# Layer-0 attention of a fused transformer kernel: ScalarE in written order, LayerNorm applied in halves, expert tiles that end at an expert's last row

## The chip, the cores and the metric

The kernel runs on one core of one Trainium2 chip. The metric is the device time of one launch in microseconds. A core has five engines with instruction streams of their own: TensorE (PE in the profile, its weight loads apart as PEld), VectorE (DVE), ScalarE (ACT), GpSimd (POOL) and SyncE (SP), which here only issues DMAs.

## What is computed

The reference has four stages over `x`, 16 sequences of 512 rows with 128 values:

```python
x = x + _L0_attn_ref(_layernorm(x), w_attn, b_attn, w_proj, b_proj)   # causal, 16 heads of 8
x = x + _L0_ffn_ref(_layernorm(x), Wg, bg, W1, b1, W2, b2)            # 8 experts, the best 2 of each row
x = x + _L1_attn_ref(_layernorm(x), w_Q, w_K, w_V)                    # full attention, 16 heads of 8
x = x + _L1_ffn_ref(_layernorm(x), w_gate, w_up, w_down)              # gated FFN on values rounded to FP4
```

In the second stage the gate takes the two largest of eight logits of a row, and only those two experts count for it.

## The kernel before

**Stages.** `attention(0)` runs the causal attention of all 16 batches and, behind each batch, the gate of the experts. It sends every row of the normalised `x` (with three more values, so `ROW` = 131 floats) to a table `x_rows` in DRAM by an indirect DMA of GpSimd, once for each of its two experts. Expert `e` owns `CAP` = 8704 rows of that table from row `e * CAP` on, and its rows lie one behind the other. `plan_tiles` then forms up to `NT` = 39 tiles of `TS` = 512 rows, and `moe`, which `attention(1)` calls, loads one tile after another with its expert's weights. `gated_ffn` ends the kernel.

**The loop of `attention(0)`.** A group is one batch and one of four sets of heads, so there are 64 groups. A group has four steps, one for each chunk `kc` of 128 keys, and a batch has 16 steps; below, "phase" is a step's place in the 16 of a batch, so phase 4 is `kc` 0 of the second group. A step issues in Python order: what hangs in `soon`; the first score matrix for the row maxima of the group three ahead (`row_max`: matmuls `ps_max`, VectorE maximum `mx`); the first score matmuls `ps_sc` with their exponentials `pt` on ScalarE (`score`, L825) and a causal mask on GpSimd; what hangs in `later`; the other half of the maxima and of the scores, for `kc` 0 and 1 only; what hangs in `last_of`; and the value matmuls `ps_av` of the step before (`attend`).

**Work hung into the steps.** For a batch two ahead the prologue has the parts `stats`, `moments`, `scale` (LayerNorm: the shift `nm` on VectorE, then four ScalarE instructions that write `xn`), `turn` (transposes, and a ScalarE copy `xnT`), `both` (for each of q and k a matmul `ps_qk` and a ScalarE instruction `hi`), `low` (VectorE, `lo`), and the spreading of q and k over strips by SP's DMAs (`first`, `second`). `put_max` transposes the maxima, ScalarE copies them to `mT` (L796), and four DMAs of SP (L798) put them into the q strips; `ps_sc` needs that. `gate_after` hangs the gate of a finished batch: `stats`, `moments`, `scale` (here ScalarE writes `xg`, L217), `turned`, the logits `ps_g`, and at every second batch a chain of small VectorE instructions that ends with the sends.

**What sets the order.** Tile's scheduler orders the instructions of each engine by priorities and its cost model, except where the kernel ties them. `in_order` ties an instruction behind the last one of its queue. TensorE is tied throughout, GpSimd mostly (its sends are `passing`: other work may pass them). `vec`, a `Lane`, ties VectorE as long as "dve" is in `strict`, which is so for `attention(0)`. ScalarE is not tied: it runs in the order that the scheduler has chosen. Two rings of PSUM buffers matter: `for_dve` (2 buffers of two banks: `ps_max`, `ps_qk`, `ps_g`, `ps_d`, `ps_n`, `ps_o`) and `for_act` (4 buffers: `ps_sc`, `ps_av`, `ps_t`, `ps_mx`, `ps_v`).

**Zero rows.** The tiles of an expert start at multiples of 512 rows, so its last tile reads past its last row. `clear_steps`, hung behind batch 13, has SP read the fill of each expert from `ends_at` and write 1536 zero rows (786 KB) behind it. The first DMA of it, of 262 KB, belongs to tiles beyond the plan.

## Time and profile before

| what | us |
|---|---|
| median of 3 runs (2483.97 to 2493.26) | 2490.11 |
| the profiled execution | 2510.72 |
| its span | 2509.0 |
| from the start to the first `ps_av` | 68.6 |
| batches 0 to 14 of `attention(0)` | 68.6 to 909.2 |
| last batch, to the last output projection | 909.2 to about 959 |
| last gate, sends and plan, to the first expert's transposes | about 959 to 996 |
| experts | 996 to about 1344 |
| `attention(1)` | to about 2208 |
| `gated_ffn` | to 2509 |

A row "A <- B: total, times, longest" of the waits gives the idle time of an engine just before instruction A that ended when B was done. A row of the timeline is start, duration, engine, line, operation, output and inputs, and in brackets the idle time before it with what ended it. A row of the windows has the busy time of each engine in a stretch, the granted clock of TensorE (1.00 is full speed) and the busy share of the DMA engines. The matmuls all have line L267 or L270 and VectorE's tied work L180, lines of helpers, so one goes by the tiles' names.

### The profile page before, as it was taken

The page shows a single profiled execution, that of the slowest core. Times are in us where ns is not written, and L with a number is a line of the kernel's source. Part 1 is how long each engine was busy: PE and PEld are TensorE (multiplying, and loading weights), DVE is VectorE, ACT ScalarE, POOL GpSimd, SP SyncE. Part 2 cuts the span into 40 slices and gives each one's busy share as a digit, 9 for nine tenths or more (in the row PEclk, how much of TensorE's full clock was granted, in tenths as well). Part 3 has the DMA queues.
Part 4 walks back from the last instruction along what each step waited for, and adds up shares of the span by engine and source line. Part 5 has one row for each costly group of instructions (what it writes and reads, how often), then busy time and mean ns, then how long its engine had stood idle before and what let it go on. Part 6 is the DMA issues. An engine that isn't in the chain of part 4 may idle for free.

```text
span 2509.0 us, 38679 instructions
## 1 busy us (share of the span) xinstructions
PE 2167.2 (86%) x13324; PEld 1077.6 (43%) x13324; DVE 1703.2 (68%) x3106; ACT 1388.2 (55%) x2716; POOL 886.1 (35%) x1384
## 2 busy tenths in 40 slices
PE   6998999999999983989998898999889999957776
PEld 2444444444444441656674333333333333325554
DVE  5666565566656546956435777777777778679887
ACT  1655555455555452333334777777777777854443
POOL 3333544445354446032002333322233331045553
PEclk8999898799999785999999999999999999978888
DMA  6112222122121255445552222222222221000000
GB/s 184 55 54 80 78 62 62 62 63 80 61 71 61 63 78 95 137 139 164 155 151 63 61 79 82 82 63 62 62 65 84 75 81 54 2 1 17 17 18 17
DMA packets 156930, 184.48 MB, mean 74 GB/s; under 512 B 25647, under 2 KB 120976, under 8 KB 148544
## 3 DMA queue, kind: packets, MB, share of 16 engines
q1 hardware_dynamic: 147806, 164.55, 23.3%
q0 software_dynamic: 8352, 17.20, 2.5%
q8 instruction: 107, 1.75, 0.3%
q14 instruction: 87, 0.71, 0.1%
q10 hardware_dynamic: 578, 0.26, 0.1%
HBM read 116.55 MB, written 63.28 MB: 72 GB/s over the span
## 4 chain that ended last, share of the span: by engine, by line
PE 65%; DVE 19%; ACT 7%; POOL 4%; issue 3%; DMA 2%; SPq 1%; POOLq 0%; ACTq 0%; DVEq 0%
PE ps_av L267 17%; PE ps_max L267 15%; PE ps_sc L267 11%; DVE mx L772 7%; PE ps_h L267 4%; PE ps_y L267 4%; ACT pt L825 3%; PE ps_qk L267 3%; PE ps_gu L267 2%; PE ps_t L270 2%; PE ps_d L270 2%; PE ps_v L267 1%; DVE q_t L1172 1%; PE ps_mx L270 1%; PE ps_o L267 1%
## 5 line engine op out<-in xcount | busy, mean ns | idle before, releaser
L772 DVE TENSOR_REDUCE mx<-ps_max 128x2 f32<-128x1024 f32 (+1 forms) x896 | 1012.7, 1147 | 436.9 <-PE ps_max L267 389.8
L825 ACT ACTIVATE pt<-ps_sc 128x512 f32<-128x512 f32 (+2 forms) x1792 | 900.3, 569 | 479.1 <-PE ps_sc L267 454.9
L267 PE MATMUL ps_sc<-q,k 64*128 64x512 f32 (+3 forms) x2048 | 485.1, 422 | 78.3 <-ACT pt L825 57.5
L267 PE MATMUL ps_av<-pt,va 128*32 128x512 f32 (+3 forms) x4096 | 503.8, 560 | 4.6 <-ACT pt L825 1.1
L267 PE MATMUL ps_max<-k,q 64*128 64x512 f32 (+3 forms) x2048 | 446.3, 453 | 33.5 <-DVE mx L772 24.5
L830 POOL TENSOR_SCALAR_AFFINE_SELECT pt<-pt 128x128 f32<-128x128 f32 (+1 forms) x768 | 248.3, 331 | 468.8 <-ACT pt L825 450.3
L267 PEld LDWEIGHTS ps_max<-k,q 64*128 64x128 f32 x2048 | 193.5, 196 | 469.1 <-issue 200.8
L267 PEld LDWEIGHTS ps_sc<-q,k 64*128 64x128 f32 x2048 | 229.6, 195 | 223.8 <-ACT pt L825 121.3
L1291 ACT ACTIVATE h<-ps_h,b1t 128x512 f32<-128x512 f32 x156 | 107.0, 687 | 194.9 <-PE ps_h L267 194.2
L267 PE MATMUL ps_h<-xT,w1t 128*128 128x512 f32 x312 | 151.3, 617 | 3.4 <-DVE xT L278 1.8
L267 PE MATMUL ps_y<-w2t,h 128*128 128x128 f32 x1248 | 148.7, 278 | 6.3 <-DVE yt L1305 6.3
L267 PEld LDWEIGHTS ps_av<-pt,va 128*32 128x32 f32 x4096 | 85.6, 111 | 146.1 <-issue 94.7
L267 PEld LDWEIGHTS ps_y<-w2t,h 128*128 128x128 f32 x1248 | 144.5, 194 | 8.9 <-DVE yt L1305 6.7
L1225 POOL DMA_INDIRECT got<-y_rows,backs x128 | 124.1, 969 | 63.0 <-issue 32.7
L532 POOL DMA_INDIRECT x_rows<-xg,slots x128 | 126.2, 986 | 27.5 <-issue 27.3
L267 PE MATMUL ps_max<-mask_bf,ident_bf 128*128 128x128 bf16 (+1 forms) x768 | 133.5, 260 | 0.0
L239 POOL TENSOR_TENSOR ln_rstd<-ln_ve,mhalf 128x4 f32<-128x4 f32 x32 | 34.5, 1078 | 255.0 <-DVE ln_nm L241 252.0
L267 PE MATMUL ps_gu<-wgT,xqT 128*128 128x352 f32 x128 | 67.0, 613 | 62.0 <-DVE hid L1418 33.2
L681 POOL TENSOR_TENSOR lo<-full,hi 128x512 fp32r<-128x512 f32 x32 | 40.9, 1280 | 150.4 <-ACT hi L679 150.4
L267 PE MATMUL ps_qk<-xnT,wp 128*128 128x512 f32 x128 | 75.8, 675 | 13.8 <-ACT hi L675 12.5
L270 PE MATMUL ps_d<-cst,av_sb 128*128 128x128 f32 x512 | 85.6, 291 | 1.4 <-ACT av_sb L856 1.4
L267 PEld LDWEIGHTS ps_h<-xT,w1t 128*128 128x128 f32 x312 | 51.2, 192 | 77.8 <-ACT h L1291 53.3
(205 smaller groups left out, 2317.5 us busy)
## 6 DMA issues: line engine op xcount, KB each, us to landing
q<-d SPq DMA_DIRECT2D x256, 128.0 KB
k<-d SPq DMA_DIRECT2D x256, 128.0 KB
d<-hi SPq DMA_DIRECT2D x64, 256.0 KB
d<-lo SPq DMA_DIRECT2D x64, 256.0 KB
xt<-x_rows SPq DMA_DIRECT2D x39, 262.0 KB
w1t<-in_w_dram SPq DMA_DIRECT2D x39, 256.0 KB
w2t<-in_w_dram SPq DMA_DIRECT2D x39, 256.0 KB
y_rows<-yt SPq DMA_DIRECT2D x39, 256.0 KB
```

Source lines behind the costliest of these rows:

```text
L239: in_order(nc.gpsimd.tensor_tensor(rstd, ve, mhalf, ALU.pow), queue="pool")
L267: return in_order(nc.tensor.matmul(out, lhsT, rhs, start=start, stop=stop))
L270: return in_order(nc.tensor.transpose(out, src, ident))
L532: ins = in_order(nc.gpsimd.indirect_dma_start(out=x_rows[:, :], out_offset=bass.IndirectOffsetOnAxis(ap=slots[:, b0 + u, k, c : c + 1], axis=0
L681: nc.gpsimd.tensor_tensor(lo, full, hi.bitcast(F32), ALU.subtract),
L772: nc.vector.tensor_reduce(hv["mx"][:, c, :, p0 : p0 + m], s4, AX.X, ALU.max),
L825: nc.scalar.activation(pt[:, 0 : m * n], ps[:, 0 : m * n], AF.Exp, scale=SCALE)
L830: nc.gpsimd.affine_select(head, head, pattern=[[0, m], [1, P]], base=0, channel_multiplier=-1, compare_op=ALU.is_ge, fill=0.0,),
L1172: nc.vector.scalar_tensor_tensor(t, r, MAGIC, v, ALU.add, ALU.add)
L1225: ins = in_order(nc.gpsimd.indirect_dma_start(out=got[:, c, :], out_offset=None, in_=y_rows[0 : min(NT, NE * (b + 1)) * TS, :], in_offset= ...
L1291: nc.scalar.activation(h[:, f, :], ps, AF.Gelu, bias=t["b1"][:, f : f + 1])
```

## The change

1. ScalarE gets a `Lane` too (`act`), and `strict` holds "act" beside "dve" in `attention(0)`: ScalarE runs in written order there.
2. `scale` becomes `shift` (VectorE's `nm`) and `apply0`, `apply1` (two ScalarE instructions each). In the prologue they hang at phases 1, 1 and 2 in place of 3; in the gate at phase 8 (after the step's last exponentials) and phase 9 in place of all at phase 8.
3. `both` issues the two matmuls `ps_qk` first and then the two `hi` (`high`), where it was matmul, `hi`, matmul, `hi`.
4. The gate's later parts are spread over more steps: the transposes at phase 11, the logits at phases 12 and 13 (were 10 and 11), the choice from phase 14 on (was 12), `fill` once for each batch, sends one step later. Four of batch 14's eight sends hang three steps earlier.
5. The start is rewritten: batch 0's LayerNorm, transposes and q, k come ahead of `pattern`, `strips` and `bias_rows`. Only batch 2's `x` is fetched before the loop; each later one is fetched in the loop, nine steps ahead of its `stats`.
6. An expert's last tile starts at its fill less 512 rows (or at 0), so it ends at its last row and overlaps the tile before. `clear_steps` goes. `clear` writes 512 zero rows at the start of each of the eight regions and of a ninth, at every second step from 6 to 22. `plan_tiles` and `places_back` get the extra arithmetic.

```diff
-    vec = Lane(nc.vector, "dve")
+    vec, act = Lane(nc.vector, "dve"), Lane(nc.scalar, "act")
...
+        def apply(part):
...
+            for c in range(NC // 2 * part, NC // 2 * (part + 1)):
+                act.activation(
                     to[:, c, 0:E], xb[:, c, :], AF.Identity,
-                    bias=nm[:, c : c + 1], scale=rstd[:, c : c + 1],
+                    bias=st["nm"][:, c : c + 1], scale=st["rstd"][:, c : c + 1],
                 )
...
-        vec.tensor_scalar(row, who[:, :, 0], float(CAP), None, ALU.mult)
-        vec.scalar_tensor_tensor(row, kth[:, :, 0], float(TS), row, ALU.mult, ALU.add)
+        vec.tensor_scalar(code, who[:, :, 0], -1.0, float(NE), ALU.mult, ALU.add)
+        vec.tensor_tensor(
+            has[:, 1 - v], rev.to_broadcast(wide), code.unsqueeze(2).to_broadcast(wide),
+            ALU.is_equal,
+        )
+        mine = pool.tile(wide, F32, name="mine", tag="xg", bufs=3)
+        vec.tensor_tensor(
+            mine, has[:, 1 - v], held.rearrange("p e o -> p o e").to_broadcast(wide), ALU.mult
+        )
+        vec.tensor_reduce(spot, mine, AX.X, ALU.add)
+        vec.tensor_scalar(spot, spot, -float(TS), 0.0, ALU.add, ALU.max)
+        vec.tensor_scalar(kth, kth, float(TS), None, ALU.mult)
+        vec.tensor_tensor(row, kth[:, :, 0], spot[:, :, 0], ALU.min)
+        vec.scalar_tensor_tensor(row, who[:, :, 0], float(CAP), row, ALU.mult, ALU.add)
...
-    def clear_steps():
...
+    def clear(e):
+
+        nc.sync.dma_start(
+            out=rows_of(x_rows, slice(e * CAP, e * CAP + TS)),
+            in_=zeros.to_broadcast([P, TS // P, ROW]),
+        )
...
-            strict.add("dve")
+            strict.update(("dve", "act"))
...
-                    nc.scalar.activation(hi, ps, AF.Identity, bias=bp[:, t : t + 1])
                     return
...
+            def high(t):
+                ps, hi, lo = st["split", t]
+                act.activation(hi, ps, AF.Identity, bias=bp[:, t : t + 1])
...
-                    both=lambda: (split(0), split(1)), low=lambda: (low(0), low(1)),
+                    both=lambda: (split(0), split(1), high(0), high(1)),
+                    low=lambda: (low(0), low(1)),
...
             run(0, "stats", "moments")
             weights_turned()
+            run(0, "shift", "apply0", "apply1", "turn", "both")
             pattern()
             strips(0)
             run(1, "stats", "moments")
+            run(0, "low", "first")
             bias_rows()
-            run(0, "scale", "turn", "both", "low", "first")
+            run(1, "shift", "apply0", "apply1", "turn", "both")
             value_columns(0)
-            run(0, "values")
             strips(1)
-            run(0, "second")
-            run(1, "scale", "turn", "both", "low")
+            run(0, "values", "second")
+            run(1, "low")
...
-            for b in range(2, B):
-                in_order(fetch(b), queue="sp")
+            in_order(fetch(2), queue="sp")
+            for b in range(3, B):
+                later.setdefault(NC * G * (b - 2) - 14, []).append(lambda b=b: fetch(b))
+            for e in range(NE + 1):
+                later.setdefault(6 + 2 * e, []).append(lambda e=e: clear(e))
...
-                    ("stats", -5, last_of), ("moments", -1, last_of), ("scale", 3, later),
-                    ("biased", 4, later), ("turn", 5, later), ("both", 7, later),
-                    ("low", 7, last_of), ("first", 9, later), ("values", 11, later),
-                    ("second", 16, later),
+                    ("stats", -5, last_of), ("moments", -1, last_of), ("shift", 1, later),
+                    ("apply0", 1, last_of), ("apply1", 2, last_of), ("biased", 4, later),
+                    ("turn", 5, later), ("both", 7, later), ("low", 7, last_of),
+                    ("first", 9, later), ("values", 10, later), ("second", 16, later),
...
+            if ng == 2:
+                steps = (
+                    (1, 2), (2, 2), (4, 1), (4, 2), (5, 2), (7, 1), (8, 2), (9, 2), (10, 0),
+                    (10, 1), (11, 1), (12, 1), (13, 1), (14, 0), (14, 1), (15, 1), (15, 1),
+                )
...
+                    if b == B - 2:
+
+
+                        at = NC * len(groups) - step + (3 if m >= len(rows) // 2 else 0)
...
+            nc.vector.tensor_scalar(held, held, -float(TS), 0.0, ALU.add, ALU.max)
```

In `steps` the first number is a distance from the step in which the batch is finished (phase 4), the second says `soon` (0), `later` (1) or `last_of` (2).

## The prediction

> **What bounds the kernel now.** I read the windows by stage first. From the first `ps_av` to the last batch TensorE is busy 778.8 of 840.6 us, VectorE 511, ScalarE 468, GpSimd 372: TensorE carries the stage, and what can be won is its 61.8 us of idle time and its clock.

> ```profile
> 68.60:909.20 840.60, 778.79 (x5545) 373.02 (x5543) 510.96 (x1065) 468.48 (x1013) 372.47 (x858) 0.90 0.21 64
> ...
> 957.60:996.00 38.40, 5.05 (x24) 3.70 (x23) 25.58 (x89) 2.44 (x6) 26.56 (x24) 0.50 0.16 48
> ```

> Next, TensorE's waits from 65 to 930 us. They sum to nearly all of that idle time, and four rows come once in each of 13 or 14 batches, always with the same length: this is no noise but one place in the schedule, met again and again.

> ```profile
> PE ps_sc L267 <- ACT pt L825: 31.0, 14, 2.2
> PE ps_qk L267 <- ACT hi L675: 10.9, 14, 0.8
> PE ps_max L267 <- DVE lo L180: 8.0, 14, 0.6
> PE ps_o L267 <- ACT aT L278: 7.3, 13, 0.6
> ```

> The timeline of batch 3 (phase 8) shows the largest. ScalarE's four `xg` stand ahead of the exponentials `pt`; they wait for `ln_nm`, which VectorE makes only after `lo` and `mx`; so `pt` is late by 2.7 + 1.65 us although its `ps_sc` was done at 247.0, and TensorE runs out of `for_act` buffers.

> ```profile
> 248.77 1.65 ACT L217 ACTIVATE xg<-x,ln_nm,ln_rstd 128x128 f32<-128x128 f32 x4 [2.68 <-DVE ln_nm L180]
> 250.33 2.05 ACT L825 ACTIVATE pt<-ps_sc 128x512 f32<-128x512 f32 x4
> ...
> 250.95 0.79 PE L267 MATMUL ps_sc<-q,k 64*128 64x512 f32 x1 [2.21 <-ACT pt L825]
> ```

> The windows around it show what follows: TensorE is busy 1.51 of 3.41 us, and then its clock is 0.50 for three such stretches. The same eight value matmuls take 1.06 us at full clock and 1.93 at half.

> ```profile
> 246.66:250.07 3.41, 1.51 (x7) 0.53 (x7) 3.21 (x5) 1.30 (x4) 0.00 (x0) 1.00 0.74 262
> 250.07:253.49 3.42, 2.54 (x15) 1.19 (x15) 0.18 (x1) 2.89 (x6) 2.10 (x5) 0.50 0.76 220
> ...
> 214.39 1.06 PE L267 MATMUL ps_av<-pt,va 128*32 128x512 f32 x8
> ...
> 256.43 1.93 PE L267 MATMUL ps_av<-pt,va 128*32 128x512 f32 x8
> ```

> Last, the ends of the stage, in the timelines of SP and TensorE. At 59.66 the four `mT` DMAs come out behind 14 fetches of `x` (11.2 us of issue) and TensorE waits 4.0 us for them; at 917.62 they stand among the zero rows and it waits 7.5 us.

> ```profile
> 48.34 11.21 SPq L84 DMA_DIRECT2D x<-in_x_dram  x14
> 59.66 2.38 SPq L798 DMA_DIRECT2D q<-mT  x4
> ...
> 911.67 5.14 SPq L384 DMA_DIRECT2D x_rows<-zeros  x3
> 917.62 5.18 SPq L798 DMA_DIRECT2D q<-mT  x4
> 924.23 20.64 SPq L384 DMA_DIRECT2D x_rows<-zeros  x5
> ...
> 931.28 1.19 PE L267 MATMUL ps_sc<-q,k 64*128 64x512 f32 x3 [7.54 <-DMA q<-mT]
> ```

> **The change part by part**, against the profiled 2510.7 us.

> 1. *`apply` in halves, behind the exponentials, ScalarE in written order.* At phase 8 no exponential stands behind `xg` any more; the next ones meet at most two of its instructions (0.9 us), while `nm` has long been made. Gone: 31.0. `xn` leaves phase 3, where it stood ahead of `aT`: gone 7.3.
> 2. *Both `ps_qk` ahead of both `hi`.* The second matmul doesn't wait for the first `hi`: gone 10.9. `lo` comes about 1.8 us sooner, but it still holds one of two `for_dve` buffers: I leave 0.4 of each 0.57 us, gone 2.4. Bounds: 0 to 8.0. Together 51.6 us.
> 3. *The clock.* A mean of 0.90 over 840.6 us is 840.6 x 0.2 = 168 us at half clock. Between the pairs 1.06/1.93 and 0.44/0.69 (two `ps_sc` of 384) I take a factor of 1.6, so each such us gives back 0.375: 63 us. Nearly every period begins in the window of the 2.2 us wait. I take four fifths as gone, 50; bounds 0 and 63. Two periods are long (416 to 465 us at 0.55, 820 to 857 at 0.54, together 78 us where two usual ones are 15): 24 us of the 63 belong to that, and explain that the profiled execution is 20.6 us above the median.
> 4. *New waits.* `ps_g` now holds a `for_dve` buffer from the end of phase 12 to phase 14, over a step with two maxima (phase 13); before it was over `kc` 3, which has one. The second `ps_max` there then waits for the first's `mx` (0.96 us less the 0.44 of `ps_sc` between, and a delay): 0.6 us, 16 times, 9.6. `ps_n` at phase 1 and the exponential of the gate (`g_d`) between two sets at phase 0 cost some 0.2 and 0.3, 8 times: 4. In all 13.6 lost; bounds 0 and 28 (twice that), as no row shows them.
> 5. *The choice from phase 14 on* takes five VectorE instructions of 0.22 us from between the two maxima of `kc` 0. VectorE has 330 us to spare: 0.
> 6. *No zero rows at the end.* The 7.5 us wait goes, and 13.7 us at half clock behind it, 13.7 x 0.375 = 5.1: 12.6. The `mT` written at 917.0 would land at about 921.8 by the 4.2 us of the first, ahead of need at 923.7.
> 7. *Zero rows at the start.* Nine DMAs of 262 KB, 0.44 us of SP each, at the 160 GB/s of the old ones 1.6 us of transfer each, one in two steps of some 5.5 us. Behind them on SP stand q and k of batch 2, needed only after the lead of three groups, 12 steps; and `mT`. Cover: that lead. 0; up to 4 if one `mT` meets them.
> 8. *Fetches in the loop.* Nine steps, over 25 us, ahead of need: 0. At the start `mT` leaves SP at once: 4.0 gone.
> 9. *The start.* `nm` waits no longer for `ps_b` and `b_bc`: ScalarE's first `xn` came at 13.09, `ln_rstd` was there at 8.4, so it can begin near 8.6, and the chain to the first `ps_max` moves by 4.5 us, with paired matmuls by some 6.5. VectorE waits 1.5 us for `rstd` with `pat`, `k` and batch 1's `stats` behind it, all of which have time before 25. Gone 6.5; bounds 3 and 8.
> 10. *The tail.* The last gate's chain (VectorE, from `x` at 958.85 to the sends at 973.84) sets it, then eight sends at 1.26 us. GpSimd now has four more sends ahead of the last `ln_rstd`, which had 2.4 us of idle: 0 to 1.3 lost. The plan gets six more small VectorE instructions (0.2 to 0.5 us each); its end already stands behind `wp`, which waits for the sends, and there such instructions took 0.2 or, beside GpSimd's memsets, 1.7 to 1.8 us. `mine` takes a third buffer of the `xg` ring, which may have to wait for the last sends. I take 2 lost; bounds -3 (`wp` placed better) and +9.
> 11. *`places_back`* gets three small instructions under the experts' matmuls (TensorE busy 323 of 344 us): 0. The number of tiles stays 39.

> Sum: 51.6 + 50 + 12.6 + 4.0 + 6.5 - 13.6 - 2 = 109, so 2510.7 - 109 = 2402 us. The median lacks most of the excess of the two long periods (0.8 x 24 = 19 of the 109): 2490.1 - 90 = **2400 us**.

> **Rivals.**
> - *The waits go, the slow clock stays* (another window per batch is too empty, at `ps_g` in phase 13 say). For it: two long periods run through windows in which TensorE is busy all the time. Against: windows busy 0.77 kept their clock. 50 and 5.1 drop out, with the 19: 2490.1 - (51.6 - 13.6 + 7.5 + 10.5 - 2) = 2436. Chance 0.13.
> - *VectorE becomes the bound*: at the new pace `ps_max` waits for `mx`, 2 us in each of 14 batches: 2428. Against: 511 us of work in some 750. Chance 0.08.
> - *Written order turns on ScalarE* (slower). If `ln_rstd` on GpSimd is late for `nm`, VectorE and ScalarE both stand, in written order, with `mx` and the exponentials behind them. In the steady batches `nm` came 4.7 to 8.4 us after `rstd`; the prologue's moves forward by two steps (2.8 + 2.4 us), so some 2 to 3 us are left, and sends of 0.97 us lie on GpSimd between. It ends slower from 90 / 14 = 6.4 us per batch on: a wait of 3.6 with a slow period of 10.2 (3.8) gives 2400 + 14 x 7.4 = 2504. Chance 0.06.
> - *The change does little*: the exponentials stay late for another reason, as the buffers of `pt`, and only start and end are won: 2490 - 23 + 14 = 2481. Chance 0.03.

> **How the numbers follow.** The likeliest case has 0.70. With all bounds good it ends at 2364; the second rival ends at 2436; the range is 2360 to 2445, which leaves out the last two. A measurement here tells about 0.5% (12 us) from no change. Faster by more 0.91, within 0.03, slower 0.06.

> **What would show it.** In the profile after, the four rows above shrink to under a fifth, except `lo`; the clock from the first `ps_av` to the last batch is 0.97 or more; a batch takes some 49 us, not 55; the first `ps_max` starts near 27 us, not 33.7; no wait for `mT` over 1 us; the experts start 36 to 40 us after the last output projection, as now. It is wrong if `ps_sc` waits for ScalarE at another phase, if `ps_max` waits more than 28 us more for `mx`, or if the clock stays at 0.90.

## The result: 2447 us, less than half of the forecast gain

| run | before, median us | after, median us | ratio, 95% interval |
|---|---|---|---|
| first comparison | 2487.11 | 2447.00 (2441.59 to 2449.80) | 0.9833, 0.9805 to 0.9861 |
| the same two kernels again (`after_again`, on the first chip of the experiments) | 2503.80 | 2484.09 (2471.27 to 2497.52) | 0.9906, 0.9871 to 0.9942 |

The change is faster by 40 us in one comparison and by 20 us in the other. The forecast was 90. 2447 lies 2 us above its range. Here and below, a ratio leaves out executions more than 1.5% above the fastest one of the same kernel.

The stages of the two profiled executions, cut at the same matmuls (first `ps_av`, last batch, last `ps_o`, first and last expert matmul, last `ps_sc` of `attention(1)`):

| stage | before | after | difference | forecast |
|---|---|---|---|---|
| start | 68.6 | 64.1 | -4.5 | -10.5 |
| batches 0 to 14 | 840.6 | 805.7 | -34.9 | -88.0 |
| last batch | 49.6 | 49.9 | +0.3 | -12.6 |
| tail (last gate, sends, plan) | 40.1 | 41.9 | +1.8 | +2.0 |
| experts | 345.2 | 343.7 | -1.5 | 0 |
| `attention(1)` | 860.8 | 833.8 | -27.0 | 0 |
| `gated_ffn` | 304.2 | 300.8 | -3.4 | 0 |

The four changed stages lose 37.3 us together, about what the medians say. The spans differ by 69.2 us, but 27.0 of that is `attention(1)`, whose instructions stand in the same order in both kernels. It took 835.2 to 835.7 us in all four kernels profiled on one chip below, and 852.0 to 856.4 us in all twelve profiled on two others: this difference doesn't belong to the change. The record doesn't name the chips of the two profiles above. Since 860.8 is near the slower group and 833.8 near the faster, they were probably not taken on one chip, and the other rows may hold a part of such a difference too: in `after_again` batches 0 to 14 took 823.1 us, 17.5 less than before and not 34.9.

The windows of the batches, after. The columns are length, then busy time and count of TensorE, its weight loads, VectorE, ScalarE and GpSimd, then granted clock, DMA share and GB/s.

```profile
64.10:869.80 805.70, 771.39 (x5543) 376.89 (x5541) 509.99 (x1058) 465.90 (x1013) 372.50 (x858) 0.90 0.22 67
```

TensorE's idle time fell from 61.8 to 34.3 us. The clock did not move: 0.896 before, 0.902 after. That is 174.6 us at half clock before and 157.8 after, and 199.4 in `after_again`. TensorE's work, 778.8 us before, takes 771.4 us.

TensorE's waits from 65 to 900 us, after:

```profile
PE ps_max L273 <- DVE lo L180: 16.1, 14, 1.1
PE ps_max L273 <- DVE mx L770: 13.4, 24, 0.7
PE ps_sc L273 <- ACT pt L180: 5.3, 7, 3.1
PE ps_sc L273 <- ACT av_sb L180: 1.8, 7, 0.3
```

The rows for `hi` and `aT` are gone, and `pt` at phase 8 with them. The row of `lo` doubled, and `mx` is new. The timeline of batch 6 shows why `lo` is late:

```profile
403.27 1.98 PE L273 MATMUL ps_qk<-xnT,wp 128*128 128x512 f32 x4
405.30 1.26 ACT L180 ACTIVATE hi<-ps_qk,bp 128x512 fp32r<-128x512 f32 x2 [1.20 <-PE ps_qk L273]
406.60 1.41 DVE L180 SCALAR_TENSOR_TENSOR lo<-ps_qk,bp,hi 128x512 fp32r<-128x512 f32 x2 [2.89 <-ACT hi L180]
408.06 0.49 PE L273 MATMUL ps_max<-k,q 64*128 64x512 f32 x2 [1.15 <-DVE lo L180]
```

The first `hi` now begins only when all four matmuls of both `ps_qk` are done, and `lo` only when both `hi` are. One wait of 1.15 us took the place of two, 0.78 for `hi` and 0.57 for `lo`. In this trace all stretches at half clock in these batches are multiples of 3.41 us long (3.4 to 20.5 us). The windows around the wait, cut in that step where the clock changes:

```profile
406.20:409.62 3.42, 2.27 (x22) 1.06 (x20) 3.02 (x5) 1.76 (x4) 0.58 (x2) 1.00 0.63 234
409.62:413.03 3.41, 3.41 (x16) 1.38 (x20) 2.64 (x3) 3.41 (x9) 1.29 (x5) 0.50 0.85 266
413.03:416.44 3.41, 3.41 (x20) 1.44 (x13) 0.92 (x1) 1.09 (x4) 0.47 (x2) 0.50 0.44 125
416.44:419.86 3.42, 3.42 (x20) 2.43 (x18) 0.85 (x3) 1.53 (x3) 0.81 (x2) 0.50 0.04 7
419.86:423.27 3.41, 3.41 (x32) 1.77 (x28) 2.05 (x8) 1.14 (x3) 0.77 (x2) 1.00 0.00 0
```

After a window with TensorE busy 0.66 (2.27 of 3.42), three windows at half clock follow, although TensorE has work all the time in them. Such a run of windows at half clock is called a slow stretch below. The 19 slow stretches of these batches begin in such places: 6 behind the wait for `lo` (which comes in 14 batches), of 10.2 us each; 8 behind the wait of 0.68 us for `mx` at phase 13 (3.4 to 20.5 us); 5 at phases 0 and 1 of every second batch, where the gate's exponential `g_d` stands between those of the scores (in four of them waits of 0.42, 0.49 and 0.23 us). Before, there were 14, all behind the 2.2 us of `pt`.

### The profile page after: what moved, and what is told of

It reads as the page before. It is cut to its first block, busy times and chain, and to the rows that moved or that the text cites. A ratio compares the mean times of both kernels' runs of the same rounds, so it can differ in the third digit from the quotient of the medians.

```text
span 2439.8 us, 38693 instructions
## 1 busy us (share of the span) xinstructions
PE 2136.8 (88%) x13324; PEld 1073.4 (44%) x13324; DVE 1705.6 (70%) x3113; ACT 1387.5 (57%) x2716; POOL 887.4 (36%) x1384
## 4 chain that ended last, share of the span: by engine, by line
PE 36%; DVE 15%; ACT 4%; POOL 3%; issue 2%; DMA 1%; SPq 0%; POOLq 0%; ACTq 0%; DVEq 0%
PE ps_av L273 10%; PE ps_max L273 7%; PE ps_sc L273 5%; DVE mx L770 4%; PE ps_h L273 4%; PE ps_y L273 4%; ACT pt L180 3%; PE ps_gu L273 2%; PE ps_qk L273 1%; DVE q_t L1179 1%; DVE q_t L1180 1%; POOL xn L259 1%; DVE q_m L1171 1%; POOL q_v L1168 1%; DVE ln_st L237 1%
## 5 line engine op out<-in xcount | busy, mean ns | idle before, releaser
L180 ACT ACTIVATE pt<-ps_sc 128x512 f32<-128x512 f32 (+2 forms) x1792 | 902.1, 568 | 475.2 <-PE ps_sc L273 464.7
L273 PE MATMUL ps_sc<-q,k 64*128 64x512 f32 (+3 forms) x2048 | 469.8, 416 | 32.4 <-ACT pt L180 29.7
L273 PE MATMUL ps_max<-k,q 64*128 64x512 f32 (+3 forms) x2048 | 439.5, 447 | 60.4 <-DVE mx L770 37.9
L273 PEld LDWEIGHTS ps_sc<-q,k 64*128 64x128 f32 x2048 | 225.4, 194 | 167.5 <-ACT pt L180 91.2
L273 PEld LDWEIGHTS ps_y<-w2t,h 128*128 128x128 f32 x1248 | 144.5, 194 | 8.2 <-DVE yt L1322 6.0
L276 PE MATMUL ps_d<-cst,av_sb 128*128 128x128 f32 x512 | 91.0, 305 | 1.4 <-ACT av_sb L180 1.4
L180 ACT COPY av_sb<-ps_av 128x512 f32<-128x512 f32 x128 | 75.4, 589 | 10.2 <-PE ps_av L273 5.8
```

Source lines behind the costliest of these rows:

```text
L180: ins = f(*args, **kw)
L273: return in_order(nc.tensor.matmul(out, lhsT, rhs, start=start, stop=stop))
L276: return in_order(nc.tensor.transpose(out, src, ident))
```

## The experiments

They ran on three chips; a ratio is always against the kernel before on the same chip (medians 2504 to 2514 on the first, 2487 on the second, 2510 on the third). "Half clock" is the time at 0.50 within batches 0 to 14 of the one execution that was profiled; for `d1_order_only` and `d2_order_halves` that was one of their longest.

| kernel | idle us, batches 0 to 14 | half clock us | slow stretches | ratio |
|---|---|---|---|---|
| before | 61.8 | 174.6 | 14 | 1 |
| `d1_order_only` / `d1_again`, ScalarE's order alone | 43.4 / 43.9 | 174.4 / 73.3 | 14 / 13 | 0.9858 / 0.9820 |
| `d2_order_halves` | 35.0 | 206.4 | 9 | 0.9903 |
| after / `after_again` | 34.3 / 35.2 | 157.8 / 199.4 | 19 / 24 | 0.9833 / 0.9906 |
| `e1_hi_between` / `e1_again` | 35.8 / 39.7 | 178.5 / 167.5 | 17 / 18 | 0.9930 / 0.9934 |
| `a1_qk_early` | 29.7 | 148.3 | 17 | 0.9841 |
| `b3_fill` | 27.1 | 118.5 | 16 | 0.9746 |
| `a2_logits_early` | 26.6 | 101.7 | 9 | 0.9701 |
| `a4_three` | 23.2 | 70.9 | 7 | 0.9557 |
| `c3_choice_back` | 21.1 | 63.4 | 5 | 0.9629 |
| `c2_qk_back` / `c2_again` | 22.5 / 23.2 | 68.5 / 60.9 | 8 / 7 | 0.9575 / 0.9573 |
| `c1_best` / `c1_again` | 18.0 / 18.0 | 3.3 / 13.3 | 0 / 1 | 0.9530 / 0.9485 |

**Moving the new waits away.** Four kernels, all on the first chip. Three are the kernel after with the steps of a few parts changed: `a1_qk_early` issues both `ps_qk` and `lo` a step sooner, `a2_logits_early` the gate's logits, and `a4_three` does both and moves the choice too. The fourth, `b3_fill`, is the kernel after with every part at its place, but with the first score matmuls of phase 8 issued three times and those of phase 13 twice into the same buffer: TensorE gets more work just where it waited, and the results are the same.

```diff
# a1_qk_early
-                    ("turn", 5, later), ("both", 7, later), ("low", 7, last_of),
+                    ("turn", 5, later), ("both", 6, later), ("low", 6, last_of),
# a2_logits_early
-  (5, 2), (7, 1), (8, 2), (9, 2), (10, 0),
+  (5, 2), (6, 1), (7, 1), (7, 2), (8, 0),
# a4_three: both of these, and
-  (10, 1), (11, 1), (12, 1), (13, 1), (14, 0),
+  (9, 2), (10, 1), (11, 1), (11, 2), (12, 0),
# b3_fill: only this, in score
+  again = {(2, 0): 2, (3, 1): 1}.get((g, kc), 0) if causal and 0 in pairs else 0
```

> The changed kernel, but both ps_qk, both hi and both lo hang one step earlier (phase 6, a step with one maximum), so that ps_qk's buffer has a whole step to come free before the next pair of maxima. Theory 1 (the slow clock follows from any window with some 0.7 to 1.1 us of waiting): the wait of ps_max for lo, 16.1 us in 14, falls under 3 us, the slow periods that begin after phase 7 (six of 10.2 us) are gone, and the time falls by 16 + 23, some 30 to 40 us below the changed kernel (ratio to the kernel before about 0.970). Theory 2 (the clock falls by its own rhythm): only the wait goes, 10 to 16 us (about 0.978), and the mean clock of the stage stays at 0.90.

Measured: 0.9841 (0.9768 to 0.9915). The wait for `lo` went from 16.1 to 5.4 us. The median is 12.3 us below that of `after_again` on the same chip, no more than the wait itself, and the intervals overlap (0.9871 to 0.9942 there). 148.3 us stayed at half clock, and all 17 stretches now begin behind waits of 0.8 us and less, for `mx` at phase 13 and around `g_d`. The 30 to 40 us of the first theory didn't come.

> The changed kernel, but the gate's transposes at phase 10 and both halves of the logits at phase 11, so that ps_g is free again before phase 13, the step with two maxima. Theory 1: the 0.68 us waits for mx at phase 13 (9 to 10 us in all) go, and with them the slow periods that begin there (about 70 us at half clock, worth 26): 25 to 35 us below the changed kernel (0.971). Theory 2: 9 us (0.980), clock 0.90.

Measured: 0.9701 (0.9627 to 0.9775). The wait for `mx` fell to 4.8 us, half clock to 101.7 us. This is where the first theory had it (0.971), and the interval is apart from that of `after_again`.

> The changed kernel with three moves: ps_qk, hi, lo one step earlier (phase 6); transposes and logits at phases 10 and 11; the gate's choice earlier, so that the exponential g_d comes at phase 15 and ps_n is free before phase 0. Theory 1: TensorE's idle time between the first ps_av and the last batch falls from 34 to under 10 us, the clock there rises from 0.90 to 0.97 or more, and the time falls by 24 + 50, 60 to 80 us below the changed kernel (0.955). Theory 2: the waits alone, 20 to 28 us (0.974), clock 0.90.

Measured: 0.9557 (0.9487 to 0.9628), where the first theory had it (0.955), though the profile fell short of it: the clock is 0.95, not 0.97, and the idle time 23.2 us, not under 10. Of that, 9.8 us is a wait that I put there: `ps_n` at phase 15 directly behind its operand `g_both`, 1.4 us in every second batch.

```profile
PE ps_n L273 <- DVE g_both L180: 9.8, 7, 1.4
```

Six of the seven slow stretches that are left begin right behind it.

> The changed kernel, but the first ps_sc matmuls of phase 8 are done three times and those of phase 13 twice, into the same buffer with the same result: useless work of 1.0 and 0.45 us put where TensorE waits 1.15 and 0.68 us. No wait is taken away. Theory 1: the windows are full, the slow periods that begin there (about 130 us at half clock) shrink by half or more, and the time falls by 15 to 40 us (0.970 to 0.977) though work is added. Theory 2: the same time as the changed kernel or up to 10 us more (0.983 to 0.987), clock 0.90.

Measured: 0.9746 (0.9670 to 0.9821), apart from the 0.9906 (0.9871 to 0.9942) of the kernel after on the same chip in a later session. So useless work won time. The repeats cover a part of the wait for `lo`, 16.1 us in the kernel after:

```profile
PE ps_max L273 <- DVE lo L180: 9.6, 14, 0.7
```

No slow stretch begins behind that wait any more, where there were 6 in after and 8 in `after_again`, and half clock fell to 118.5 us. The waits for `mx` at phase 13, still 0.5 to 0.63 us, go on starting stretches. (The idle time in the table counts the repeats as work.)

**All of it.** `c1_best` is `a4_three` with the choice placed so that `g_both` is ready for `ps_n`, with the zero rows and the fetches of `x` (and the last of the four `mT` DMAs) tied into SP's queue at their written places, and with batch 14's gate one step later and its sends later by up to three.

```diff
+  (9, 2), (10, 1), (10, 2), (11, 2), (12, 0),
...
-        nc.sync.dma_start(
+        in_order(nc.sync.dma_start(
...
+        ), queue="sp", passing=True)
...
+                    lambda b=b: in_order(fetch(b), queue="sp", passing=True)
...
+            if b == B - 2:
+                steps = tuple((d + (i > 1), w) for i, (d, w) in enumerate(steps))
```

> The kernel with all waits found moved: both ps_qk a step earlier, the router's logits a step earlier, the choice with its exponential and its reduction at 10 to 12 (so that ps_n has its operand at 15), the zero rows and fetches at their written places in the queue of SP, the last batch but one's gate steps one later, its sends later. Theory that the clock follows windows in which TensorE is short of work: idle in batches 0 to 14 below 16 us, slow clock there below 50 us, start 5 to 6 us shorter, last batch 3 to 4 shorter: 2380 us on a chip where before takes 2514, ratio 0.946, within 0.938 to 0.953. Rival, VectorE or ScalarE now carries the batch: no better than the three moves without these, ratio 0.956 or more. Rival on the last batch, later steps only move the wait: last batch 45 us as with the three moves.

Measured: 0.9530 (0.9469 to 0.9592), 2359.92 us, at the upper end of the expected range, with 18.0 us idle instead of under 16; again on the third chip:

> c1_best on the chip of the next three. Theory that the clock follows windows with waits: 0.953, within 0.947 to 0.957, under 20 us at half clock in batches 0 to 14. Rival, the clock there was a property of the other chip: slow stretches in the batches here too, 0.958 or more.

Measured: 0.9485 (0.9440 to 0.9530), 2378.28 us. The windows and then TensorE's waits of `c1_again` (60 to 800 us):

```profile
60.00:787.40 727.40, 709.38 (x5545) 353.08 (x5544) 503.57 (x1060) 461.99 (x1013) 370.40 (x857) 0.99 0.27 81
```

```profile
PE ps_max L273 <- DVE lo L180: 5.4, 14, 0.4
PE ps_n L273 <- DVE g_both L180: 4.3, 7, 0.6
PE ps_qk L273 <- DVE mx L770: 4.2, 14, 0.3
```

Against the profile of after, which is probably from another chip, this is 16 us less idle time, but 78 us less length (805.7 to 727.4): as many matmul records (5545 and 5543) take 709.4 us instead of 771.4. No window at full clock had TensorE busy under 0.80; those of 0.82 kept their clock, and the one slow stretch, of 10.2 us, follows a window that was busy throughout, so waits are not the only cause. VectorE, busy 504 us of 727, is still no bound. The last batch took 42.8 us. This version beats both kernels.

**The price of one wait.** From `c1_best`, one edit is taken back at a time: `both` and `low` at phase 7 again (`c2`), or the choice at steps 10 to 14 again (`c3`).

> The best kernel (c1_best) with one move taken back: both ps_qk, hi and lo at phase 7 again, so that TensorE waits 1.15 us for lo once in 14 batches (16 us instead of 5.4 and 4.2). Theory that a window with one such wait starts a slow stretch of some 10 us in every second batch: idle 6 us more, some 70 us at half clock in batches 0 to 14 (at 0.375 some 26 us), 32 us in all, ratio 0.013 above c1_best, about 0.966. Rival, the clock follows the sum of the waits over a batch, which is small here: 6 us, ratio about 0.955.

Measured, on the first chip: 0.9575 (0.9527 to 0.9622), nearer the rival's 0.955 than the theory's 0.966; but `c1_best` had not run on this chip, so that its 0.9530 is no sure base.

> One wait of 1.15 us a batch put back into c1_best. Theory: 5 us of idle, 8 or so slow stretches, some 65 us at half clock more, 20 to 30 us in all: ratio 0.008 to 0.012 above c1_again. Rival, only the idle counts: 0.002 above.

Measured, beside `c1_again`: 0.9573 (0.9523 to 0.9624), median 18.6 us above it, inside the theory's 0.008 to 0.012. The intervals of the ratios touch at their ends, but none of the five times of the one kernel (2376.5 to 2385.0) reaches the five of the other (2391.7 to 2411.0). Idle time rose by 5.2 us, half clock by 47.6. Every one of its seven stretches begins behind the wait for `lo`; the windows of one:

```profile
223.97:227.39 3.42, 2.27 (x20) 0.94 (x18) 2.88 (x5) 1.77 (x4) 2.12 (x4) 1.00 0.65 236
227.39:230.80 3.41, 3.41 (x20) 1.54 (x20) 2.79 (x3) 3.37 (x9) 1.27 (x5) 0.50 0.88 288
230.80:234.21 3.41, 3.41 (x19) 1.26 (x12) 0.74 (x1) 1.17 (x4) 1.52 (x3) 0.50 0.58 162
234.21:237.63 3.42, 3.42 (x16) 3.16 (x16) 1.04 (x3) 1.67 (x3) 1.79 (x3) 0.50 0.02 5
237.63:241.04 3.41, 3.41 (x35) 1.99 (x34) 1.73 (x8) 1.24 (x3) 0.76 (x2) 1.00 0.06 20
```

> c1_best with the choice of the experts back at steps 10 to 14, where the exponential stands between those of the scores and ps_g is held over phase 13: waits of 0.4 to 0.8 us on mx and pt return, 13 us or less. Theory that windows with waits of 0.7 us begin slow stretches too (of 3 to 7 us, in two of three batches): 30 us and more, ratio 0.012 above c1_again. Rival, the clock stands such short waits and only those over 1 us drop it: the idle alone, 0.003 to 0.005 above.

Measured: 0.9629 (0.9581 to 0.9678), 37.1 us above `c1_again`, the intervals apart. In the profiles, whose batches 0 to 14 differ by 28.5 us, only 3.1 us of that is idle time: the same matmuls take 734.7 us instead of 709.4.

```profile
60.40:816.20 755.80, 734.73 (x5544) 363.76 (x5543) 504.63 (x1058) 462.90 (x1013) 370.46 (x858) 0.96 0.26 78
```

Its stretches begin behind still shorter waits. Two windows, and the waits in the first of them:

```profile
297.77:301.18 3.41, 2.75 (x24) 1.33 (x24) 3.31 (x8) 2.06 (x6) 1.95 (x5) 1.00 0.47 137
301.18:304.59 3.41, 2.92 (x23) 1.02 (x19) 1.95 (x5) 2.09 (x6) 1.14 (x5) 0.50 0.61 184
```

```profile
299.15 0.44 PE L273 MATMUL ps_max<-k,q 64*128 64x384 f32 x2 [0.24 <-DVE mx L770]
...
299.85 0.21 ACT L180 ACTIVATE g_d<-g_d 128x8 f32<-128x8 f32 x1 [1.34 <-DVE g_d L180]
...
300.60 0.44 PE L273 MATMUL ps_sc<-q,k 64*128 64x384 f32 x1 [0.42 <-ACT pt L180]
```

After two waits that sum to 0.66 us this window was 0.81 full, and the clock fell for 17 us.

**The parts of the change by themselves.** `d1_order_only` is the kernel before with nothing but ScalarE tied into written order; all other engines issue the same instructions in the same order. `d2_order_halves` adds the halves, at the places of the change but for the second half of the gate's `xg`: that one hangs ahead of the scores of phase 9, not behind them. `e1_hi_between` is the kernel after with the first `hi` between the two pairs of `ps_qk` again.

```diff
# d1: as in the change
+    vec, act = Lane(nc.vector, "dve"), Lane(nc.scalar, "act")
+            strict.update(("dve", "act"))
# d2: besides
+                    ("shift", 1, later), ("apply0", 1, last_of), ("apply1", 2, last_of),
+                    (4, 1, shift), (4, 2, apply0), (5, 0, apply1),
# e1
-   both=lambda: (split(0), split(1), high(0), high(1)),
+   both=lambda: (split(0), high(0), split(1), high(1)),
```

> The kernel before with one thing of the change: ScalarE's instructions keep the order they are written in during attention 0. All other engines issue the very same order as before; no halves, no earlier matmuls, zero rows as before. Theory of the prediction (order by itself costs and gains nothing, only the places do): ratio 1.000, within 0.995 to 1.005, TensorE's four rows of waits in the batches as before within a third. Rival, a written order turns on ScalarE by itself: over 1.006, with new waits for pt. Second rival, the order is the gain: 0.985 or less.

Measured: 0.9858 (0.9764 to 0.9953). That is two of its four executions; the median of all four against that of all before gives 0.9896, so this run leaves the size open.

> ScalarE's written order alone, once more. The first profile had the wait for pt at 12.4 us instead of 31.0 and the slow clock as before: theory from that, the waits alone: ratio 0.992, within 0.988 to 0.996. The prediction's zero for the order alone: 1.000. Rival, it is most of the change: 0.985.

Measured: 0.9820 (0.9760 to 0.9880), faster than expected and near the rival's 0.985. Order alone gives about as much as the whole change did (0.9833 and 0.9906), though the two never ran side by side on one chip. Its waits, from 65 to 870 us, and the place itself in batch 3:

```profile
PE ps_sc L267 <- ACT pt L180: 12.4, 14, 0.9
PE ps_qk L267 <- ACT hi L180: 10.9, 14, 0.8
PE ps_max L267 <- DVE lo L180: 8.0, 14, 0.6
PE ps_o L267 <- ACT aT L180: 7.3, 13, 0.6
```

```profile
241.67 1.09 ACT L180 ACTIVATE pt<-ps_sc 128x512 f32<-128x512 f32 x2 [1.02 <-PE ps_sc L267]
243.33 1.65 ACT L180 ACTIVATE xg<-x,ln_nm,ln_rstd 128x128 f32<-128x128 f32 x4 [0.57 <-DVE ln_nm L180]
...
245.51 0.69 PE L267 MATMUL ps_sc<-q,k 64*128 64x384 f32 x1 [0.90 <-ACT pt L180]
```

The scheduler's order had put the four `xg` ahead of all the step's exponentials. In written order two of these come first, and the wait shrinks from 2.2 to 0.9 us: 18.6 us less in all. A stretch still begins in nearly every batch, but those of this profile last only 3.4 or 6.8 us. What sets the length is open: with the same waits the profile of `d1_order_only`, on another chip, has four stretches of 27 to 41 us and 174.4 us at half clock, not 73.3. So two profiles that differ by 100 us at half clock can still be of one kernel, and a single row of the table above proves little by itself.

> The kernel before with ScalarE in written order and the LayerNorm values in halves at the places of the change; both ps_qk are not ahead of hi, values, choice, fetches, zero rows as before. Prediction's step 1 with its share of the clock (38 us of waits and some 37 of the 50 us of clock): ratio 0.970. Theory now, waits go but slow stretches begin at the shorter waits that stay (hi and lo at phases 7 and 8, places of phases 13 to 15): some 38 us or less, ratio 0.983 to 0.988, with over 130 us at half clock in batches 0 to 14.

Measured: 0.9903 (0.9873 to 0.9933), slower than both forecasts. The waits for `pt` and `aT` are gone, 20 us, and `ps_t` waits for `xg` in their place (11.2 us in 27 waits), which the kernel after, with its later places, doesn't have. On the chip of both runs the medians of all executions are 2460.97 us for order alone and 2460.34 with these halves: no time was won. What the halves give at exactly the places of the change was not measured.

> The kernel after with step 2 undone: the first hi is written between the two pairs of ps_qk again, TensorE's order is unchanged. Prediction's step 2 (10.9 us of waits for hi and 2.4 of lo come back, and their clock with them): some 20 us slower than after, ratio about 0.992. Theory now (one wait of 1.15 us a batch replaced two that made 1.35): as after, ratio 0.983 within 0.006, the row of lo shorter, and the row ps_qk waiting for hi back at 8 to 12 us.

Measured: 0.9930 (0.9904 to 0.9955). No chip is on record for after's 0.9833, so again with the kernel after beside it:

> The kernel after as it is, on the chip of the next three, so that they can be set against it. Both theories: ratio 0.983, within 0.978 to 0.988.

> Step 2 undone once more, beside the kernel after on one chip (the first run's ratio 0.993 was from another chip). Prediction's step 2 (13 us of wait and its clock, some 20 us): 0.008 above after. Theory that step 2 gave nothing, since one wait of 1.15 us stands for two of 0.78 and 0.57: within 0.003 of after.

Measured: after 0.9906 (0.9871 to 0.9942), outside its expected 0.978 to 0.988, `e1_again` 0.9934 (0.9911 to 0.9957), 4.9 us apart in the medians with overlapping intervals. Step 2 was worth little, perhaps nothing; the 20 us of the forecast are excluded only loosely.

**The start.** `b2_start` is the kernel after with the zero rows, the fetches and the last `mT` DMA tied into SP's queue (the second part of `c1_best`). In the kernel after, the program wrote them 6 steps or more behind the start, but nothing tied them, and the scheduler put them at its head:

```profile
6.80 4.51 SPq L386 DMA_DIRECT2D x_rows<-zeros  x6
...
12.80 3.21 SPq L386 DMA_DIRECT2D x_rows<-zeros  x2
...
20.44 0.38 SPq L693 DMA_DIRECT2D d<-hi  x1
...
26.63 2.44 SPq L702 DMA_DIRECT2D q<-d  x4
```

```profile
34.69 0.79 PE L273 MATMUL ps_max<-k,q 64*128 64x512 f32 x2 [6.07 <-DMA q<-d]
```

> The kernel after with the zero rows and the x fetches held at their written places in the queue of SP, behind the fetches of d and q of the first batches. Theory that the copies written 6 steps or more later were issued at the head of the queue and made d and q late: the first ps_max at 28 to 29 us instead of 34.7, start 5 to 6 us shorter, ratio 0.002 below after. Rival, the start is bound by something else (the copies of pat, the strips): first ps_max earlier but the first ps_av as in after, ratio as after.

The same issue of q and the first `ps_max` in `b2_start`:

```profile
19.96 2.49 SPq L702 DMA_DIRECT2D q<-d  x4
```

```profile
27.72 0.49 PE L273 MATMUL ps_max<-k,q 64*128 64x512 f32 x2 [0.47 <-DVE lo L180]
...
33.18 0.69 PE L273 MATMUL ps_max<-k,q 64*128 64x384 f32 x2 [4.09 <-DVE mx L770]
```

The first `ps_max` moved by 7.0 us; 4.1 of that went into a new wait for VectorE, and the start became 4.2 us shorter than that of `after_again` (60.1, 64.3; 5 to 6 were expected). The ratio, 0.9875 (0.9822 to 0.9928), can't tell that from 0.9906.

## Why the prediction failed, step by step

**Step 3, the clock, is the step that failed.** It took 50 of 63 us as gone, on two grounds: that nearly every slow period began in the window of the 2.2 us wait, and that windows busy 0.77 kept their clock. Both were true of batches 0 to 14 of the one profile. The second is no rule: in the same profile's `attention(1)` windows busy 0.77 (2.62 of 3.41 us, from 1564.2 and 1673.4 us on) were followed by half clock, and in after, windows of the batches busy 0.80 lost their clock 8 times. Over the 18 profiles of this study, windows of 3.41 us at full clock in batches 0 to 14 were followed by half clock so often:

| TensorE busy | windows | followed by half clock |
|---|---|---|
| under 0.60 | 19 | 19 |
| 0.60 to 0.75 | 124 | 96 |
| 0.75 to 0.90 | 473 | 95 |
| over 0.90 | 2893 | 7 |

The change emptied the window that had always lost its clock (busy 0.34 to 0.56 before, 14 of 14) and left or made others in the two middle rows. What came was 174.6 - 157.8 = 16.8 us less at half clock, by the step's own 0.375 some 6 us and not 50 (TensorE's work became 7.4 us shorter); in `after_again` it was 24.8 us more. The factor itself was low rather than high: from `c1_again` to after TensorE's busy time grows by 62.0 us for 144.5 us more at half clock, 0.43, and a straight line through all profiles but `b3_fill` has 0.45. That the clock is what was missing, and that waits of 0.4 to 1.2 us can hold it down, is shown by `c1_again`, `c2_again` and `c3_choice_back` on one chip, and by `b3_fill`. What decides within the middle rows is not shown: in `e1_hi_between` waits of 0.78 and 0.57 us started no stretch, and 0.68 at phase 13 started one in nearly every batch; and a window of 0.81 lost its clock in `c3_choice_back` where those of 0.82 in `c1_again` kept it.

The same step explained the 20.6 us by which the profiled execution exceeded the median by two long slow periods in the batches, and the sum took 19 us off for it. The profile's `attention(1)`, some 25 us longer than the 835.2 to 835.7 us on the chip where before's median is also 2487, fits a difference of chips better. Which of the two it was stays open.

**Step 2, mis-sized.** The 10.9 us for `hi` went. For `lo` 5.6 us were to be left and there are 16.1: I counted on a `lo` that comes 1.8 us sooner, but its ScalarE input waits for both matmul pairs, 2.0 us. This 10.5 us is the whole excess of idle time in the batches: 61.8 - 51.6 + 13.6 = 23.8 forecast, 34.3 measured.

**Step 1, right in its waits.** `pt` at phase 8 and `aT`, 38.3 us, are gone. 18.6 of that is order alone, and the halves as placed in `d2_order_halves` brought no time beyond it.

**Step 4, right in size and under-priced.** 13.4 us for `mx` and 2.2 for `pt` at `g_d`, 13.6 forecast. I charged the waits and not their clock. `c3_choice_back` puts the choice part of them back, and with 3.1 us more idle time the batches take 28.5 us longer.

**Steps 7 to 9, the start.** 10.5 us were forecast, 4.5 came. ScalarE's first `xn` did begin early, but step 7 costed the zero rows at their written places; moved to the head of SP's queue they held d and q: with them ahead, the first d is issued at 20.44 us and q at 26.63. With the written places (`b2_start`) these are 17.66 and 19.96, and the first `ps_max` is at 27.7 us, where step 9 had it (27). The step failed in taking the program's order for the queue's.

**Step 6, the last batch.** The 7.5 us wait went (idle 11.4 to 6.4 us), and a new one of 3.1 us came, in the last batch's timeline:

```profile
891.38 0.36 DVE L180 SCALAR_TENSOR_TENSOR ln_nm<-ln_mv,ln_rstd 128x4 f32<-128x4 f32 x1 [1.68 <-POOL ln_rstd L206]
891.78 1.65 ACT L180 ACTIVATE xg<-x,ln_nm,ln_rstd 128x128 f32<-128x128 f32 x4 [1.49 <-DVE ln_nm L180]
...
893.96 0.52 PE L273 MATMUL ps_sc<-q,k 64*128 64x512 f32 x1 [3.12 <-ACT pt L180]
```

Batch 14's gate leaves one step, not two, from `moments` to `shift`; `ln_rstd` is late for `nm`, and ScalarE stands with the exponentials behind it: the rival "written order turns on ScalarE", in one place out of sixteen. The clock fell from 0.806 to 0.746 there, and none of the 12.6 us came. With that gate one step later the last batch took 42.8 us in `c1_best`; other moves of that kernel act there too (44.9 us in `a4_three` without this one), so its share is not shown apart.

**Steps 5, 8, 10, 11** held: VectorE 510 us as before, no wait for `mT`, tail +1.8 (2 forecast), experts -1.5.

**The rivals.** What happened is the first one, the waits go and the slow clock stays, and the place it names, `ps_g` in phase 13, is among the three that did it. It had 0.13. That its 2436 lies so near the measured 2447 is partly luck: it forecast a gain of 54 us, and the two comparisons gave 40 and 20.

## What to carry to other kernels

Where a clock follows short windows, as in the table above, count the windows in which TensorE is short of work, not the sum of the waits: a change that halves the waits and leaves one short window in each batch may get little of the clock back (here 61.8 to 34.3 us idle, 174.6 to 157.8 us at half clock), and in `c1_again` 16 us less of waits went with 78 us less in length. A place in the schedule that did not drop the clock in one profile is no proof that it can't (the wait for `lo` came in 14 batches of after and started a stretch in 6), so price each new wait with its slow stretch as well. What is written late in a program but tied to nothing can be issued first: look where the scheduler puts it before costing it at nothing.

## What the runs showed of the hardware

Windows whose waits summed to 0.66 us (`c3_choice_back`, 297.77 to 301.18 us) to 1.15 us (after, 406.20 to 409.62 us) lost the clock, and the longest gap of TensorE in batches 0 to 14 of any kernel here was 2.2 us (before; 1.15 after, 0.49 in `c3_choice_back`). A window at half clock in which TensorE was busy did not always bring the full clock back: of 590 such windows busy over 0.97 in the 18 profiles, 219 were followed by full clock, and one stretch in the kernel before lasted 44.4 us. `attention(1)`, the same instructions throughout, had 8 slow stretches on one chip and 12 to 15 on the two others, and 16 to 21 us lie between their lengths.
